# A four-layer network on one core: filler matmuls, earlier centre copies, later x copies and a lent PSUM bank in the scan layer

## The chip, the core and the metric

The kernel runs on one core of one Trainium2 chip. The time is that of one launch on the device in microseconds (us); a comparison uses the median of several runs. The profiles are one profiled execution each: PE is TensorE's matmuls, PEld its weight loads, DVE is VectorE, ACT is ScalarE, POOL is GpSimd, and SP is the engine from whose queue the scan layer's DMAs are issued. "L1800" is line 1800 of the kernel.

## What is computed

The input `x` has shape 3 x 256 x 48 x 48 in float32. Four layers follow one another, each of the form `x = x + layer(groupnorm(x))`: an attention block, a convolution whose weights are mixed per image, a plain 3x3 convolution, and a selective state-space scan (Mamba). The change is in the fourth layer. With L = 2304 tokens per image it is, cut to what matters:

```
xn = layernorm(tokens, over channels) * norm_w + norm_b
x_in, z = split(xn @ in_proj_w.T)               # 512 channels each
u  = silu(conv1d(x_in, 4 taps per channel) + conv_b)
dt_raw, B, C = split(u @ x_proj_w.T)            # 16, 16, 16
dt = softplus(dt_raw @ dt_proj_w.T + dt_proj_b)
for each token t:                               # 16 states per channel
    h = h * exp(dt_t * A) + dt_t * B_t * u_t
    y_t = sum over states of h * C_t
y   = (y + u * D) * silu(z)
out = y @ out_proj_w.T                          # 256 channels
```

## The kernel before, in words

**Chunks, steps and parts.** Of each image's 2304 tokens 384 are a chunk (CH), so there are 3 x 6 = 18 chunks. The 512 inner channels are four groups of 128 (m = 0 to 3), the 16 states of a channel two halves (h = 0, 1). A pair (m, h) is a step, so that a chunk has 8 steps, called 0 to 7 here (step = 2m + h); "steps five to eight" of the change are steps 4 to 7 in this count. A step has 8 parts, each one scan of 128 rows by 384 tokens. There are 18 x 8 x 8 = 1152 scans. "Scan (2, 3)" is part 3 of step 2, and so for the exponentials.

**What one part does.** `scan` (L1797) is one VectorE instruction (L1800). It multiplies the running state by the decay in a PSUM slot and adds the tile `hs`. The decay is `exp(dt * A)`, written by ScalarE in `decay` (L1784, instruction L1792). There are three slots, so the exponential for a part is issued three parts ahead, after the scan that frees its slot: after scan (2, 0) follows exponential (2, 3).

**What one step does.** At its end `fill` (L1754) writes the inputs `dt * u * B` of the next step into `hs`. VectorE writes the upper part (`fill_upper`, L1745, instruction L1748) and reads `dt * u` from a PSUM tile of two banks that TensorE has spread over the rows (`spread_pe`, L1712). GpSimd writes the rest (L1762, L1766) from rows that DMAs have spread (`spread`, L1693; `spread_second`, L1704). Then GpSimd multiplies the finished states by C (`times_c`, L1804, instruction L1817), and TensorE adds them up one step later (`add_states`, L1822). `gate` (L1839) multiplies the sum by silu(z) on VectorE. `spread_pe` runs at the end of even steps and has one tile: the banks are written at the end of step 2m - 2, both are read at the end of step 2m - 1, and the first one once more at the end of step 2m.

**What is threaded in between.** All other work of the layer is cut into small stages that run beside the scans of other chunks. Three lists say where: `plan` (L1381) for the chunks one and two ahead, `gating` (L1430) for z, `after` (L1418) for the chunk before. An entry `(j, place, rel, stage)` runs `stage` for chunk `at + rel` in half step j (j = 2 x step + part // 4) at a place: BEGIN, MID, DONE and LATE are after the first, second, third and fourth scan of the half step, and PE_ is after LATE in its first half and after `fill` and `times_c` in its second. Within a place the order is `after`, `plan`, `gating`, `last_of_all`. The lines that matter:

- `group_scale` (L1210), `less_mean` (L1218: TensorE, both shared banks), `centre` (L1233: two ScalarE copies L1235 out of the banks and a Square L1237), `square_mean` (L1227), `inverse_root` (L1239: Ln L1241 and Exp L1242), `normalise` (L1244, VectorE), `tokens` (L1248): the layer norm of the chunk two ahead, in steps 6 and 7.
- `project_x` (L1261), `take_x` (L1268: ScalarE copy L1269), `taps` (L1271: 8 records L1273), `take_u` (L1278: ScalarE L1281), in steps 0 to 2, and `silu` (L1285) over u in step 3. `silu` over z is `last_of_all`, at (3, LATE). Each silu is a table load, the pass over 1536 columns (L1286) and a table load back (L229).
- `project_u`, `take_dbc`, `project_dt` (L1315), `softplus`, `take_dt` (L1331: VectorE L1334, L1335), `keep_dt` (L1337: ScalarE copies L1339 and two stores), in steps 4 to 6.
- `project_z`, `take_z` (L1354, L1357) in steps 6 and 7 and at the start of the next chunk.
- `residual` (L1368), `project_y` (L1359: 10 records, L1361 and L1363), `store` (L1372: ScalarE copy L1373 and a DMA): the output of the chunk before. It is made in two halves of 128 channels.

All stages share two PSUM banks, `bank[0]` and `bank[1]` (L1206): each product lies there until ScalarE or VectorE has taken it.

**What sets the order.** TensorE, VectorE, ScalarE and GpSimd run the layer's instructions in program order (`keep_order`, L1906). An instruction that waits holds up all behind it on its engine. SP's DMAs are ordered by the framework and wait for their own semaphores; they are often issued well ahead of the compute beside them. The loop over steps and parts is at L1853 to L1890, the end of the layer (last sum, gate, output) at L1892 to L1901.

Of the kernel before, what the change touches and what calls it, by code (L numbers as in the profile page):

```python
# [16 lines left out]
P = 128  # L17
# [8 lines left out]
CH = 384  # L26
# [9 lines left out]
DI = 4  # L36
# [48 lines left out]
def net(  # L85
# [21 lines left out]
    nc = tc.nc  # L107
# [14 lines left out]
    def v(name, i=0, n=1):  # L122
# [3 lines left out]
    ident = const.tile([P, P], F32, name="ident")  # L126
# [6 lines left out]
        out=gview, in_=gview, pattern=[[-8, 16], [0, 8]], compare_op=ALU.is_ge,  # L133
# [3 lines left out]
        out=gview, in_=gview, pattern=[[8, 16], [0, 8]], compare_op=ALU.is_ge,  # L137
# [243 lines left out]
    with ExitStack() as l0:  # L381
# [36 lines left out]
        with ExitStack() as p1:  # L418
# [15 lines left out]
            for b in ORDER:  # L434
# [100 lines left out]
        with ExitStack() as p2:  # L535
# [9 lines left out]
            for i in range(NB):  # L545
# [501 lines left out]
        i = NB - 1  # L1047
# [151 lines left out]

    class Chunk:  # L1200
        def __init__(self):
            self.second = {}


    whole = [psg.tile([P, 512], F32, name=f"ps_g{j}") for j in range(2)]
    bank = [t[:, :CH] for t in whole]  # L1206
# [61 lines left out]
    def take_x(k, m):  # L1268
        nc.scalar.copy(w3v["xi"][:, m % 3, :], whole[m % 2][:, :XH])  # L1269

    def taps(k, m):  # L1271
        for tap in range(DCONV):
            nc.tensor.matmul(  # L1273
                bank[m % 2], w3v["taps"][:, m, tap, :], w3v["xi"][:, m % 3, tap : tap + CH],
                start=tap == 0, stop=tap == DCONV - 1,
            )

    def take_u(k, m):  # L1278
        if m == 0:
            k.u = room(k, "u")  # L1280
        nc.scalar.activation(  # L1281
            k.u[:, m, :], bank[m % 2], AF.Identity, bias=v("conv_b", m)
        )
# [39 lines left out]
    def softplus(k, m0):  # L1323
# [4 lines left out]
        nc.scalar.activation(both, both, AF.Exp, scale=-1.0)  # L1328
        nc.scalar.activation(both, both, AF.Ln, bias=1.0)

    def take_dt(k, m0):  # L1331
        for j in range(2):
            m, pdt = m0 + j, bank[j]
            nc.vector.scalar_tensor_tensor(pdt, pdt, 0.0, k.dt[:, m, :], ALU.max, ALU.add)  # L1334
            nc.vector.tensor_tensor(k.dtu[:, m, :], pdt, k.u[:, m, :], ALU.mult)  # L1335

    def keep_dt(k, m0):  # L1337
        for j in range(2):
# [17 lines left out]
            k.sz = room(k, "sz")  # L1356
        nc.scalar.copy(k.sz[:, m, :], bank[j])  # L1357

    def project_y(k, mo, lo=0, hi=DI):  # L1359
        if lo == 0:  # L1360
            nc.tensor.matmul(bank[mo], ident, k.ot[:, mo, :], start=True, stop=False)  # L1361
        for m in range(lo, hi):
            nc.tensor.matmul(  # L1363
                bank[mo], w("out", m * 256 + mo * P, P), k.sz[:, m, :],
                start=False, stop=m == DI - 1,
            )

# [2 lines left out]
        nc.sync.dma_start(k.ot, xd[k.b][:, :, k.c * CH : (k.c + 1) * CH])  # L1370

    def store(k, mo):  # L1372
        nc.scalar.copy(k.ot[:, mo, :], bank[mo])  # L1373
        nc.sync.dma_start(
            out[k.b, mo * P : (mo + 1) * P, k.c * CH : (k.c + 1) * CH], k.ot[:, mo, :]
        )
# [3 lines left out]
    BEGIN, MID, DONE, LATE, PE_ = range(5)  # L1380
    plan = [  # L1381
        (12, MID, 2, group_scale),
        (12, PE_, 2, less_mean),
        (13, LATE, 2, centre),
        (13, PE_, 2, square_mean),
        (14, MID, 2, inverse_root),
        (15, MID, 2, normalise),
# [8 lines left out]
        (2, DONE, 1, lambda k: project_x(k, 2)),  # L1396
        (2, LATE, 1, lambda k: take_u(k, 1)),
        (2, LATE, 1, lambda k: project_x(k, 3)),
        (3, LATE, 1, lambda k: take_x(k, 2)),
        (3, LATE, 1, lambda k: taps(k, 2)),  # L1400
        (4, BEGIN, 1, lambda k: take_x(k, 3)),
        (4, BEGIN, 1, lambda k: taps(k, 3)),
        (4, DONE, 1, lambda k: take_u(k, 2)),
        (5, MID, 1, lambda k: take_u(k, 3)),
        (7, LATE, 1, lambda k: silu(k.u)),
        (8, BEGIN, 1, project_u),
        (8, LATE, 1, take_dbc),
# [11 lines left out]
        (0, MID, 0, lambda k: k.at and take_z(k, 2, 0)),  # L1419
        (0, MID, 0, lambda k: k.at and take_z(k, 3, 1)),  # L1420
        (2, MID, -1, residual),
        (5, BEGIN, -1, lambda k: project_y(k, 0)),
        (6, MID, -1, lambda k: store(k, 0)),
        (7, PE_, -1, lambda k: project_y(k, 1)),
        (8, MID, -1, lambda k: store(k, 1)),
    ]

    last_of_all = [(3, LATE, 0, lambda k: silu(k.sz))]

# [246 lines left out]
    with ExitStack() as l3:  # L1676
# [35 lines left out]
        def spread_pe(k, m):  # L1712

            t = psr.tile([P, 2, 512], F32, name="ps_r")
            for q in range(2):
                r = slice(32 * q, 32 * q + 32)
                nc.tensor.matmul(
                    t[:, q, :CH], rep[r].rearrange("p r d -> p (r d)"), k.dtu[r, m, :],
                    start=True, stop=True,
                )  # L1720
            k.ps = t


        steps = [(at, m, h) for at in range(len(todo)) for m in range(DI) for h in range(2)]
        tiles = {}
        state = {}

        parts_of_step = [(g, q) for a in range(2) for g in range(2) for q in (2 * a, 2 * a + 1)]
        slots = [psd.tile([P, 512], F32, name=f"ps_da{i}") for i in range(3)]
# [54 lines left out]
        def decay(n):  # L1784

            s, part = divmod(n, 8)
            if s >= len(steps):
                return
            at, m, h = steps[s]
            g, q = parts_of_step[part]  # L1790
            col = (m * 4 + 2 * h + g) * 4 + q
            nc.scalar.activation(  # L1792
                slots[n % 3][:, 1 : CH + 1], chunks[at].rows[m][0][:, q, :], AF.Exp,
                scale=amat[:, col : col + 1],
            )
# [49 lines left out]
        k = chunks[0]  # L1845
# [7 lines left out]
        for s, (at, m, h) in enumerate(steps):  # L1853
            if m == 0 and h == 1 and at + 2 <= last:
                fetch(at + 2)
            for part in range(8):
                j = 4 * m + 2 * h + part // 4
                scan(s, part)
                decay(8 * s + part + 3)
                if part == 0 and h == 0:  # L1860
                    c, n = (at, m + 1) if m + 1 < DI else (at + 1, 0)
                    if c <= last:
                        rows = getattr(chunks[c], "rows", {})
                        chunks[c].rows = {**rows, n: spread(chunks[c], n)}
                if part == 4 and h == 1 and s + 1 < len(steps):
                    spread_second(chunks[steps[s + 1][0]], steps[s + 1][1])
                if part == 4 and s + 1 < len(steps):
                    first_states(s + 1)
                if part % 4 == 0:
                    run(at, j, BEGIN)  # L1870
                if part % 4 == 1:
                    run(at, j, MID)
                if part % 4 == 2:
                    run(at, j, DONE)
                if h == 1 and part == 7 and s >= 3:
                    gate(*steps[s - 3][:2])
# [139 lines left out]
```

## Time and profile before

| | |
|---|---|
| time, median of 3 runs | 3412.58 us (3409.98 to 3416.41) |
| the profiled execution, its own time | 3411.51 us |
| its span, first to last instruction | 3409.8 us |
| its scan stage, first to last scan | 2018.1 to 3389.4 us |
| VectorE busy from 2018.0 to 3389.4 us | 1318.6 of 1371.4 us |
| GpSimd busy there | 1271.2 us |
| ScalarE busy there | 1101.1 us |
| TensorE busy there, mean granted clock | 1091.5 us, 0.87 |
| after the last scan, to the end | 20.4 us |

A line of the timeline gives start, duration, engine, source line, operation, output<-inputs and shape, how many equal instructions are merged, and in brackets the engine's idle time before and what ended it. The view of waits sums such brackets by who waited for whom. The view by windows gives each engine's busy time in stretches of time, and "PEclk", the share of full speed that TensorE was granted. A float32 matmul of the kernel's text appears as two records, each with its own weight load.

### The profile page before, as it was taken

What the parts mean: (1) busy time and instruction counts of PE and PEld (TensorE: products, weight loads), DVE (VectorE), ACT (ScalarE), POOL (GpSimd) and SP (SyncE); (2) the same over time, 40 slices, a digit from 0 to 9 for tenths busy, and PEclk for the clock granted to TensorE, in tenths of its full rate; (3) what the DMA queues carried; (4) which work ended last, traced back from release to release, by engine and by line L of the source; (5) the groups of instructions that cost most, each with busy time, mean ns of one, the idle gap of its engine ahead of it and who ended that gap; (6) DMA issues with size and microseconds to landing.
All of it is one profiled execution on the core that took longest, in us unless ns stands there. A gap on an engine that the chain in (4) does not pass through costs nothing.

```text
span 3409.8 us, 52160 instructions
## 1 busy us (share of the span) xinstructions
PE 3047.4 (89%) x19882; PEld 1442.5 (42%) x19882; DVE 2902.4 (85%) x3302; ACT 2381.6 (70%) x3596; POOL 1335.5 (39%) x457
## 2 busy tenths in 40 slices
PE   7999999999999999979999987878888888878785
PEld 4334343453333435547677753333333333333331
DVE  3799889959989996479966369999999999999998
ACT  2688888848888885332233558888888888888874
POOL 0000000000000000210000039999899999999897
PEclk8999999999999999989999998888889898988887
DMA  4000000010000002756501144545555454545552
GB/s 167 28 8 10 8 8 7 12 42 5 8 10 8 7 8 80 238 171 222 199 22 38 42 116 110 120 115 139 141 126 131 121 122 121 128 114 136 137 133 54
DMA packets 182152, 290.65 MB, mean 85 GB/s; under 512 B 34737, under 2 KB 148465, under 8 KB 179970
## 3 DMA queue, kind: packets, MB, share of 16 engines
q1 hardware_dynamic: 168658, 267.15, 29.0%
q10 hardware_dynamic: 13232, 20.06, 1.8%
q8 instruction: 158, 2.59, 0.3%
q14 instruction: 104, 0.85, 0.1%
HBM read 236.24 MB, written 50.64 MB: 84 GB/s over the span
## 4 chain that ended last, share of the span: by engine, by line
PE 59%; DVE 21%; ACT 11%; DMA 4%; issue 3%; POOL 1%; SPq 1%; ACTq 0%; DVEq 0%; POOLq 0%
PE ps_s L638 16%; PE acc L651 14%; DVE hs L1800 13%; PE ps_c L1533 8%; PE ps_g L1273 3%; PE ps_g L1222 3%; ACT ps_da L1792 2%; DVE u L296 2%; PE ps_y L462 2%; PE ps_m L665 1%; PE ps_s L1031 1%; PE ps_m L711 1%; PE ps_y L1834 1%; PE ps_g L1349 1%; ACT L229 1%
## 5 line engine op out<-in xcount | busy, mean ns | idle before, releaser
L642 ACT ACTIVATE pt<-ps_s 128x1024 f32<-128x1024 f32 x972 | 942.6, 1022 | 154.5 <-PE ps_s L638 141.8
L1800 DVE TENSOR_TENSOR_SCAN hs<-ps_da,hs 128x385 f32<-128x385 f32 x1152 | 1006.6, 940 | 47.4 <-ACT ps_da L1792 45.8
L857 DVE TENSOR_TENSOR part<-part,pt 128x2048 f32<-128x2048 f32 x396 | 906.8, 2290 | 41.2 <-ACT pt L642 18.4
L1792 ACT ACTIVATE ps_da<-dtr,u 128x384 f32<-128x384 f32 x1152 | 657.0, 583 | 201.7 <-DVE hs L1800 191.0
L164 POOL TENSOR_TENSOR rstd<-ve,mhalf 128x2 f32<-128x2 f32 (+1 forms) x26 | 16.4, 631 | 1476.5 <-DVE ve L162 1476.5
L638 PE MATMUL ps_s<-q,kt 32*128 32x512 f32 (+1 forms) x4320 | 576.4, 592 | 0.1
L651 PE MATMUL acc<-pt,vt 128*32 128x512 f32 (+1 forms) x4320 | 520.9, 561 | 0.2
L1533 PE MATMUL ps_c<-vt,u 128*128 128x288 f32 x1728 | 432.5, 411 | 21.0 <-DVE u L263 21.0
L1817 POOL TENSOR_TENSOR hc<-hs,x 128x3072 f32<-128x3072 f32 x72 | 405.3, 5629 | 5.4 <-DVE hs L1800 5.2
L1817 POOL TENSOR_TENSOR hc<-hs,bc 128x3072 f32<-128x3072 f32 x71 | 399.8, 5631 | 11.0 <-DVE hs L1800 7.9
L1533 PEld LDWEIGHTS ps_c<-vt,u 128*128 128x128 f32 x1728 | 331.0, 192 | 117.6 <-issue 19.8
L638 PEld LDWEIGHTS ps_s<-q,kt 32*128 32x128 f32 x4320 | 195.3, 183 | 199.1 <-issue 120.2
L1834 PE MATMUL ps_y<-hc,u 128*32 128x384 f32 x2304 | 252.0, 562 | 17.3 <-POOL hc L1817 17.3
L651 PEld LDWEIGHTS acc<-pt,vt 128*32 128x32 f32 x4320 | 94.4, 108 | 353.4 <-issue 326.7
L1273 PE MATMUL ps_g<-u 128*128 128x384 f32 x576 | 199.5, 494 | 21.0 <-ACT u L1269 20.9
L1766 POOL TENSOR_TENSOR hs<-dtur,x 128x1536 f32<-128x1536 f32 x72 | 209.2, 2905 | 7.2 <-DMA dtur<-dtud 7.2
L1766 POOL TENSOR_TENSOR hs<-dtur,bc 128x1536 f32<-128x1536 f32 x72 | 209.6, 2911 | 0.0
L1318 PE MATMUL ps_g<-wconv,u 17*128 17x384 f32 x144 | 79.2, 684 | 106.7 <-ACT x L1339 81.0
L1273 PEld LDWEIGHTS ps_g<-u 128*128 128x128 f32 x576 | 107.0, 190 | 110.5 <-ACT u L1269 42.2
L1222 PE MATMUL ps_g<-wconv,u 128*128 128x384 f32 x144 | 85.6, 765 | 64.6 <-ACT x L1339 64.1
L1834 PEld LDWEIGHTS ps_y<-hc,u 128*32 128x32 f32 x2304 | 65.4, 119 | 178.8 <-issue 152.6
L1549 ACT COPY cb<-ps_c 128x288 f32<-128x288 f32 x48 | 19.2, 399 | 158.4 <-PE ps_c L1533 144.2
(251 smaller groups left out, 3842.5 us busy)
## 6 DMA issues: line engine op xcount, KB each, us to landing
wconv<-in_we SPq DMA_DIRECT2D x144, 384.0 KB, 4.2
dtr<-dtd SPq DMA_DIRECT2D x288, 192.0 KB, 4.0
dtur<-dtud SPq DMA_DIRECT2D x288, 96.0 KB, 4.2
wconv<-xd SPq DMA_DIRECT2D x36, 384.0 KB, 4.9
x<-bcd SPq DMA_DIRECT2D x72, 192.0 KB, 5.3
dtd<-x SPq DMA_DIRECT2D x36, 384.0 KB, 3.5
dtuq<-dtud SPq DMA_DIRECT2D x288, 48.0 KB, 2.2
bc<-bcd SPq DMA_DIRECT2D x72, 192.0 KB, 5.1
```

The lines of the kernel that those rows point to most:

```text
L638: nc.tensor.matmul(s[:, j, cols], kt[r, mt * P : (mt + 1) * P], q[r, :n], start=True, stop=True,)
L642: nc.scalar.activation(p[:, h0 : h0 + 2, :], s, AF.Exp)
L651: nc.tensor.matmul(acc[h * HD : (h + 1) * HD, :n], vt[:, mt, g * P + h * HD : g * P + (h + 1) * HD], p[:, h, cols], start=mt == 0, stop=mt ...
L857: ): nc.vector.tensor_tensor(part, first, p, ALU.add)
L1222: nc.tensor.matmul(bank[to], w3v["less"][:, int(to != ct), :], k.xg[:, ct, :], start=ct == 0, stop=ct == CT - 1,)
L1273: nc.tensor.matmul(bank[m % 2], w3v["taps"][:, m, tap, :], w3v["xi"][:, m % 3, tap : tap + CH], start=tap == 0, stop=tap == DCONV - 1,)
L1533: nc.tensor.matmul(pc[:, :HN], u[:, i, dy, ct, m * P : (m + 1) * P], vt[:, i, ct, dy * TW : dy * TW + HN], start=ct == 0 and dy == 0, stop ...
L1766: nc.gpsimd.tensor_tensor(states(s)[:, :, 2:4, 1:], chunks[at].rows[m][1].unsqueeze(1).broadcast_to([P, 2, 2, CH]), b_rows(s, 0, 2), ALU.mult,
L1792: nc.scalar.activation(slots[n % 3][:, 1 : CH + 1], chunks[at].rows[m][0][:, q, :], AF.Exp, scale=amat[:, col : col + 1],)
L1800: nc.vector.tensor_tensor_scan(b, slots[(8 * s + part) % 3][:, : CH + 1], b, 0.0, ALU.mult, ALU.add)
L1817: nc.gpsimd.tensor_tensor(hc, tiles[s][:, :, :, 1:], cb.broadcast_to([P, 2, 4, CH]), ALU.mult)
L1834: nc.tensor.matmul(k.y_ps[32 * q : 32 * q + 32, :CH], fold, hc[:, g, q, :], start=False, stop=h == 1 and g == 1,)
```

## The change

- **Fillers.** `keep_busy(src, times)` issues matmuls of 128 columns with the identity as weights. Nobody reads their results. They go to columns 384 to 511 of the two banks of the current spread tile, alternately. They stand at `take_dt` (3 after each product `dtu`, once a spread tile exists), after scan (4, 3): 4; after scans (5, 1), (5, 2), (5, 3), (5, 5): 3 each; after scans (6, 0), (6, 1), (6, 2): 3, 3, 2; and 5 between `less_mean` and `square_mean`, at (13, PE_). Each of the fillers behind a scan reads what that scan wrote.
- **Centre.** `centre` moves from (13, LATE) to (13, DONE), one part earlier.
- **x copies.** `take_x` and `taps` of m = 2 move from (3, LATE) to (4, BEGIN), behind z's silu; those of m = 3 from (4, BEGIN) to (4, DONE). `take_u` of m = 2 moves from (4, DONE) to (5, LATE), of m = 3 from (5, MID) to (6, LATE).
- **First output half.** `project_y(k, 0)` moves from (5, BEGIN) to (4, BEGIN) and is written to the second bank of the spread tile instead of `bank[0]`; its `store` moves from (6, MID) to (5, DONE).
- **Spread rows.** `spread_second` moves from part 4 to part 0 of odd steps.

```
+    def keep_busy(src, times):
+        for i in range(times if spread_tiles else 0):
+            nc.tensor.matmul(
+                spread_tiles[-1][:, i % 2, CH:], ident, src, start=True, stop=True
+            )
...
     def take_dt(k, m0):
...
             nc.vector.tensor_tensor(k.dtu[:, m, :], pdt, k.u[:, m, :], ALU.mult)
+            keep_busy(k.dtu[:, m, :P], 3)
...
-    def project_y(k, mo, lo=0, hi=DI):
+    def project_y(k, mo, lo=0, hi=DI, into=None):
         if lo == 0:
-            nc.tensor.matmul(bank[mo], ident, k.ot[:, mo, :], start=True, stop=False)
+            k.y_out[mo] = bank[mo] if into is None else into
+            nc.tensor.matmul(k.y_out[mo], ident, k.ot[:, mo, :], start=True, stop=False)
...
     def store(k, mo):
-        nc.scalar.copy(k.ot[:, mo, :], bank[mo])
+        nc.scalar.copy(k.ot[:, mo, :], k.y_out[mo])
...
-        (13, LATE, 2, centre),
+        (13, DONE, 2, centre),
+        (13, PE_, 2, lambda k: keep_busy(ident, 5)),
         (13, PE_, 2, square_mean),
...
-        (3, LATE, 1, lambda k: take_x(k, 2)),
-        (3, LATE, 1, lambda k: taps(k, 2)),
-        (4, BEGIN, 1, lambda k: take_x(k, 3)),
-        (4, BEGIN, 1, lambda k: taps(k, 3)),
-        (4, DONE, 1, lambda k: take_u(k, 2)),
-        (5, MID, 1, lambda k: take_u(k, 3)),
+        (4, BEGIN, 1, lambda k: take_x(k, 2)),
+        (4, BEGIN, 1, lambda k: taps(k, 2)),
+        (4, DONE, 1, lambda k: take_x(k, 3)),
+        (4, DONE, 1, lambda k: taps(k, 3)),
+        (5, LATE, 1, lambda k: take_u(k, 2)),
+        (6, LATE, 1, lambda k: take_u(k, 3)),
...
-        (5, BEGIN, -1, lambda k: project_y(k, 0)),
-        (6, MID, -1, lambda k: store(k, 0)),
+        (4, BEGIN, -1, lambda k: project_y(k, 0, 0, DI, lent[0])),
+        (5, DONE, -1, lambda k: store(k, 0)),
...
     def spread_pe(k, m):
...
             k.ps = t
+            lent[0] = t[:, 1, :CH]
+            spread_tiles[:] = [t]
...
+        busy = {(2, 0, 3): 4, (2, 1, 1): 3, (2, 1, 2): 3, (2, 1, 3): 3, (2, 1, 5): 3,
+                (3, 0, 0): 3, (3, 0, 1): 3, (3, 0, 2): 2}
...
                 scan(s, part)
                 decay(8 * s + part + 3)
+                if (m, h, part) in busy:
+                    g, q = parts_of_step[part]
+                    keep_busy(tiles[s][:, g, q, 1 : P + 1], busy[m, h, part])
...
-                if part == 4 and h == 1 and s + 1 < len(steps):
+                if part == 0 and h == 1 and s + 1 < len(steps):
                     spread_second(chunks[steps[s + 1][0]], steps[s + 1][1])
```

More of the change, by code (lines that the diff above doesn't have):

```diff
@@ L1201, in __init__ @@
         def __init__(self):
-            self.second = {}
+            self.second, self.y_out = {}, {}
     whole = [psg.tile([P, 512], F32, name=f"ps_g{j}") for j in range(2)]
@@ L1329, in softplus @@
         nc.scalar.activation(both, both, AF.Ln, bias=1.0)
+    spread_tiles = []
+    def keep_busy(src, times):
[3 more added lines that the diff above has]
+            )
     def take_dt(k, m0):
@@ L1357, in take_z @@
         nc.scalar.copy(k.sz[:, m, :], bank[j])
-    def project_y(k, mo, lo=0, hi=DI):
+    def project_y(k, mo, lo=0, hi=DI, into=None):
         if lo == 0:
-            nc.tensor.matmul(bank[mo], ident, k.ot[:, mo, :], start=True, stop=False)
+            k.y_out[mo] = bank[mo] if into is None else into
+            nc.tensor.matmul(k.y_out[mo], ident, k.ot[:, mo, :], start=True, stop=False)
         for m in range(lo, hi):
             nc.tensor.matmul(
-                bank[mo], w("out", m * 256 + mo * P, P), k.sz[:, m, :],
+                k.y_out[mo], w("out", m * 256 + mo * P, P), k.sz[:, m, :],
                 start=False, stop=m == DI - 1,
@@ L1426, in net @@
     ]
+    lent = [None]
     last_of_all = [(3, LATE, 0, lambda k: silu(k.sz))]
```

## The prediction

> **What bounds the kernel now.** I read the busy table by windows first: from the first to the last scan (1371.4 us) VectorE is busy for 1318.6. So the stage is VectorE's, and all that a schedule can win is its idle time, 53 us. The view of waits of VectorE in that stage says whose it is; I then looked up each such wait in the timeline.
>
> ```profile
> DVE hs L1800 <- ACT ps_da L1792: 45.8, 50, 1.4
> ```
>
> 50 waits of a scan for its exponential, 45.8 us. They stand at three places of a chunk: before scan (2, 3), 1.13 us in 17 chunks (18.7 in all); before (7, 3), 1.38 and 0.3 in turn in 16 chunks (14.0); before (7, 5), 0.75 in 16 chunks (12.2). First step 2, ScalarE, then VectorE:
>
> ```profile
> 2494.90 0.59 ACT L1792 ACTIVATE ps_da<-dtr,u 128x384 f32<-128x384 f32 x1 [0.27 <-DVE hs L1800]
> 2496.22 0.48 ACT L1269 COPY u<-ps_g 128x387 f32<-128x387 f32 x1 [0.74 <-PE ps_g L1263]
> 2496.72 1.28 ACT L1286 ACT_TABLE_LOAD   x1
> 2498.01 1.49 ACT L1286 ACTIVATE x<-x 128x1536 f32<-128x1536 f32 x1
> 2499.52 1.28 ACT L229 ACT_TABLE_LOAD   x1
> ...
> 2500.92 0.58 ACT L1792 ACTIVATE ps_da<-dtr,u 128x384 f32<-128x384 f32 x1
> ```
> ```profile
> 2497.75 2.66 DVE L1800 TENSOR_TENSOR_SCAN hs<-ps_da,hs 128x385 f32<-128x385 f32 x3
> 2501.53 2.77 DVE L1800 TENSOR_TENSOR_SCAN hs<-ps_da,hs 128x385 f32<-128x385 f32 x3 [1.13 <-ACT ps_da L1792]
> ```
>
> Exponentials (2, 2) and (2, 3) are 6.0 us apart. Between them lie z's silu, a copy of x, and ScalarE's wait of 0.74 for the matmuls behind that copy. Three slots let ScalarE lead by three scans; that isn't enough. Then step 7 (ScalarE, TensorE, VectorE):
>
> ```profile
> 2544.72 0.58 ACT L1792 ACTIVATE ps_da<-dtr,u 128x384 f32<-128x384 f32 x1 [0.26 <-DVE hs L1800]
> 2545.77 0.48 ACT L1235 COPY wconv<-ps_g 128x384 f32<-128x384 f32 x1 [0.46 <-PE ps_g L1222]
> 2547.05 0.48 ACT L1235 COPY wconv<-ps_g 128x384 f32<-128x384 f32 x1 [0.80 <-PE ps_g L1222]
> 2547.56 0.84 ACT L1237 ACTIVATE wconv<-wconv 128x768 f32<-128x768 f32 x1
> ...
> 2548.40 1.09 ACT L1792 ACTIVATE ps_da<-dtr,u 128x384 f32<-128x384 f32 x2
> 2550.05 0.56 ACT L1241 ACTIVATE ps_g<-ps_g,epst 128x384 f32<-128x384 f32 x1 [0.56 <-PE ps_g L1229]
> ```
> ```profile
> 2541.52 5.49 PE L1222 MATMUL ps_g<-wconv,u 128*128 128x384 f32 x8 [4.17 <-ACT x L1339]
> 2548.45 0.91 PE L1229 MATMUL ps_g<-wconv,mean 128*128 128x384 f32 x2 [1.45 <-ACT wconv L1237]
> ```
> ```profile
> 2549.08 1.81 DVE L1800 TENSOR_TENSOR_SCAN hs<-ps_da,hs 128x385 f32<-128x385 f32 x2 [1.38 <-ACT ps_da L1792]
> 2551.64 0.96 DVE L1800 TENSOR_TENSOR_SCAN hs<-ps_da,hs 128x385 f32<-128x385 f32 x1 [0.75 <-ACT ps_da L1792]
> ```
>
> The centre copies wait for `less_mean`, 8 records in 5.49 us, 0.64 apart; at full clock records of this size are 0.32 apart. The windows view shows why: after TensorE's pauses of steps 5 and 6 the granted clock is half.
>
> ```profile
> 2523.25:2536.90 13.65, 9.63 (x38) 2.97 (x30) 13.40 (x18) 10.97 (x23) 13.14 (x4) 0.50 0.41 98
> 2540.30:2547.10 6.80, 5.49 (x8) 2.52 (x8) 6.80 (x10) 4.77 (x11) 4.01 (x3) 0.50 1.08 249
> ```
>
> (Columns after the length: PE, PEld, DVE, ACT and POOL busy, then the clock.)
>
> **What the Trainium skill says.** (1) "TensorE: Matmul & The Clock Gate", section "What's actually happening": TensorE runs at half clock after an idle window of about 3.4 us and at full clock after a busy one. The trace agrees: 0.64 against 0.32 us per record, and stretches of a multiple of 3.4 us. (2) "PSUM — Partial Sum Buffer", section "PSUM bank collisions raise a hardware error": two engines must be kept apart by bank, not by address. So I take a filler and the `fill_upper` that reads another part of its bank to be ordered by a wait. No pair in this trace shows it. (3) "ScalarE: Activation LUTs", "What ACT_TABLE_LOAD costs": about 1283 ns a load; here 1.28.
>
> **Part by part.**
>
> *x copies behind the silu.* Exponential (2, 2) ends at 2495.49. Without copy and wait the table load starts at 2495.5, 1.2 us sooner, and exponential (2, 3) ends at 2500.3 instead of 2501.5. VectorE is ready at 2501.53 - 1.13 = 2500.40. The wait falls from 1.13 to 0.1. The copy (0.47) now stands behind (2, 3): (2, 4) ends about 2501.2, when VectorE wants it; the second copy, after (2, 5), has 0.4 us of slack. I leave 0.1 us per chunk (ends 0 and 0.4): **17 x 1.0 = 17 us won**.
>
> *Output half in the lent bank, taps, later u copies.* TensorE's work in step 2 is the same, in another order: sums (from 2497.3 to 2499.4), `project_y` 10 x 0.32 to 2502.6, taps 8 x 0.32 each to 2505.2 and 2507.8. Those who take the results come later: the store's copy at about 2504.4, the u copies at 2505.4 and 2508.6. The lent bank was last read by `fill` at the end of step 1 and is next written by the spread at the end of step 2, behind the taps, at about 2509 as before (2509.5); it is needed 4 us later. Cost 0; without that slack the u copies would hold ScalarE for tenths. The residual's DMA gets behind `spread_second` on SP, hence behind GpSimd's L1762 (2485.6): it lands by 2493 for use at 2499.4. Nothing. The store's own DMA only moves forward.
>
> *Spread rows sooner.* Their four issues stood behind a store of step 5 and eight loads of B and C; GpSimd waited 4.5 us for them in step 6 (59.9 and 22.5 us in all by the waits view). VectorE didn't: L1766 ends at 2546.8 and its first reader is scan (7, 4) at 2549.96. Worth 0 directly, but it gives GpSimd (71.3 us of work in 76.4 us) the room for a shorter chunk. On SP the stores of `keep_dt` get behind these issues, which wait for GpSimd's L1762: done by 2521.1, the stores are ready at 2530.8. Nothing.
>
> *Fillers.* A filler is two records of 128 columns: a third of 0.32, so 0.11 us each if streaming binds; 0.19 each if the weight load does (a load of 128 columns has a mean of 190 ns in group L1273). So 3 fillers are 0.6 to 1.1 us. To count activity I take streaming time times the share of the array used. In the trace, windows of 3.4 us under about 0.25 turned the clock down, those over 0.3 didn't, and 0.7 turned it up. The pauses get 3 x 0.21 = 0.64 us after nearly every scan: six groups in step 5 and five in step 6, at most 1.8 us apart except around the sums of step 4's states, which are 1.9 us of work themselves (2 x 0.32 and 4 x 0.32). Every window then holds 0.4 or more by this count. I take the clock to stay up. Then `less_mean` ends 2.6 us sooner (8 x 0.32).
>
> A filler waits for its scan or product, and all of TensorE's queue behind it with it: `project_dt` and `less_mean`. Both wait longer for ScalarE's copies of the banks; the last fillers before `less_mean` follow scan (6, 2), which ends at 2540.4, so they end 0.4 us before it can start. But `fill` at the end of step 5 reads both their banks: `project_dt` from 2530.45, 4 records to 2532.0, 3 fillers to 2532.6 to 2533.1; `fill` starts at 2533.13, with all of step 6's scans behind it on VectorE. I take 0.05 us, ends 0 and 0.3: **1 us lost**.
>
> *Centre one part earlier.* Exponential (7, 1) ends at 2544.47. `less_mean` gives its banks by 2544.4, so copies and Square (1.75 us) run without a wait to 2546.1, (7, 2) ends at 2546.65; VectorE wants it at 2546.77. The margin is 0.1 us. (7, 3) ends at 2547.3, wanted 2547.6. **All of 14.0 us won.** Next late is (7, 5): it stands behind Ln and Exp (0.98 us), which wait for `square_mean`, 1.6 us after its start (2548.45 to 2550.05). Square ends at 2546.1, but the five fillers in front start only after `fill` has read their bank (2545.1) and take 1.1 to 1.9 us, to 2546.3 to 2547.0; `square_mean`, z's product and the next sums queue behind them. So Ln starts at 2547.9 to 2548.6, (7, 5) ends at 2549.5 to 2550.2, wanted 2549.3. I take 0.5 left of 0.75 (ends 0.2 and 0.9): **4 us won** (ends +9 and -2).
>
> Sum: 17 + 14 + 4 - 1 = 34 us. The profiled execution took 3411.5 (span 3409.8 and 1.7 around it): 3377.5. The median of the runs is 1.1 above it: **3378.6 us**. With all ends good it is 3371, with all bad 3394. The 20.4 us after the last scan hold no edit.
>
> **Rivals.**
>
> *All hidden.* If a filler's record takes 0.11 us and starts ahead of `fill`'s read, Ln isn't held up: nearly all 45.8 us go, 3367.
>
> *Step 7 keeps its waits.* For: the margin of 0.1 us at (7, 2), and five fillers ahead of `square_mean`. What is won at (7, 3) comes back at (7, 2) and (7, 5); step 2 alone remains: 3412.6 - 17 = 3396.
>
> *The clock stays down, and the change costs time.* One mechanism, at the pauses of steps 5 and 6: fillers count for too little, and a window under a quarter halves the clock. Then `less_mean` frees its second bank at 2547.05, as before; Square ends at 2548.4, (7, 2) at 2549.0 against 2546.8, so 2.2 in one phase, 1.3 in the other (where the clock had risen halfway), instead of 0.85 at (7, 3). Fillers at half clock (0.43 or more) and `square_mean` (4 x 0.64) add about 1.1 at (7, 5). So 16 x (0.9 + 1.1) = 32. `fill` of step 5 waits for `project_dt` to 2533.2 and 3 fillers to 2534.5: 17 x 1.4 = 24. Less 17 from step 2: 3412.6 + 39 = 3452. Against it: the counted windows. It decides from 0.25 down.
>
> *No effect.* GpSimd, with 5 us to spare per chunk, becomes the bound and returns what VectorE wins: 3411. Against it: its wait for rows goes.
>
> **Chances.** As forecast 0.60, all hidden 0.13, step 7 keeps its waits 0.15, clock down 0.09, no effect 0.03. The likeliest case alone reaches from 3371 to 3394; the range for 8 in 10 takes in the two cases beside it, 3364 to 3400. A measurement of this kernel can tell about 0.2% (7 us) from no change. Faster 0.88, same 0.03, slower 0.09.
>
> **What would show it.** Right: no wait over 0.15 us before scan (2, 3) and none at (7, 3); a clock of 1.00 all through steps 4 to 7; `less_mean` in 2.9 us; some 0.5 us left at (7, 5); GpSimd's wait for `dtuq` gone. Wrong: waits before scan (7, 2), a `fill` of VectorE waiting for TensorE, windows at 0.50, waits for GpSimd's `hs`.

## The result, and the profile after

| | before | after |
|---|---|---|
| median of 4 runs each | 3411.28 us | 3373.68 us (3369.03 to 3375.2) |
| ratio, 95% interval | | 0.9885 [0.9869, 0.99] |
| the profiled execution | 3411.51 us | 3369.03 us |
| its layers ahead of the scans | 2018.1 | 2013.8 |
| its scan stage, start of the first to end of the last scan | 1371.3 | 1330.8 |
| from there to the end | 20.4 | 22.7 |

37.6 us are won by the medians. The profiled execution of after happens to be the shortest of its four runs. Of its 42.5 us, 4.3 lie in layers whose code is unchanged: in all the executions shown here the first scan starts anywhere from 2012.9 to 2022.0 us. So each kernel below is read by its ratio and by its scan stage. The stage is shorter by 40.5 us.

From L1331 on, line numbers move by up to 17: the scan is L1817 now, the exponential L1809, `fill_upper` L1765, GpSimd's fills L1779 and L1783, the store's copy L1384, a filler L1336. The view of waits of VectorE, from 2000 us on, shows who waited for whom, us in all, how often and the longest:

```profile
DVE sz L1858 <- PE ps_y L1851: 7.8, 1, 7.8
DVE hs L1765 <- ACT wconv L1384: 3.6, 17, 0.2
...
DVE ps_g L1343 <- ACT x L1329: 3.0, 17, 0.2
...
DVE hs L1817 <- ACT ps_da L1809: 2.4, 3, 1.6
```

50 waits of 45.8 us for an exponential have become 3 of 2.4, all in the first chunk; waits of 0.09 us that remain at (7, 5), too short for this view, come to 1.4 us more. The first line is the gate after the last scan. The second is new: 17 waits of `fill_upper` for the store's copy.

**Step 2 after the change**, ScalarE, then VectorE, in the timeline of one chunk:

```profile
2476.69 0.58 ACT L1809 ACTIVATE ps_da<-dtr,u 128x384 f32<-128x384 f32 x1 [0.27 <-DVE hs L1817]
2477.29 1.28 ACT L1286 ACT_TABLE_LOAD   x1
2478.59 1.48 ACT L1286 ACTIVATE x<-x 128x1536 f32<-128x1536 f32 x1
2480.09 1.28 ACT L229 ACT_TABLE_LOAD   x1
2481.38 0.20 ACT L1799 COPY gmat<-hs 128x8 f32<-128x8 f32 x1
2481.49 0.58 ACT L1809 ACTIVATE ps_da<-dtr,u 128x384 f32<-128x384 f32 x1
...
2485.76 0.58 ACT L1809 ACTIVATE ps_da<-dtr,u 128x384 f32<-128x384 f32 x1 [0.27 <-DVE hs L1817]
2486.28 0.47 ACT L1384 COPY wconv<-ps_r 128x384 f32<-128x384 f32 x1
```
```profile
2479.55 7.02 DVE L1817 TENSOR_TENSOR_SCAN hs<-ps_da,hs 128x385 f32<-128x385 f32 x8
2486.78 0.56 DVE L1765 TENSOR_TENSOR hs<-ps_r,x 128x384 f32<-128x384 f32 x1 [0.21 <-ACT wconv L1384]
```

The table load follows exponential (2, 2) at once, (2, 3) starts 4.8 us after (2, 2) instead of 6.0, and the eight scans run without a gap. But the last scan ends at 2486.57, the store's copy only at 2486.75, and `fill_upper` starts 0.03 us after that. `fill_upper` reads the first bank of the spread tile, the copy the second, where the output half now lies.

**Step 7 after the change**, TensorE, ScalarE, VectorE:

```profile
2522.40 2.85 PE L1222 MATMUL ps_g<-wconv,u 128*128 128x384 f32 x8 [0.31 <-ACT x L1349]
2526.07 1.38 PE L1336 MATMUL ps_r<-ident 128*128 128x128 f32 x10 [0.83 <-DVE hs L1765]
2527.29 1.46 PE L1229 MATMUL ps_g<-wconv,mean 128*128 128x384 f32 x4
```
```profile
2524.75 0.58 ACT L1809 ACTIVATE ps_da<-dtr,u 128x384 f32<-128x384 f32 x1 [0.27 <-DVE hs L1817]
2525.27 0.85 ACT L1235 COPY wconv<-ps_g 128x384 f32<-128x384 f32 x2
2526.15 0.84 ACT L1237 ACTIVATE wconv<-wconv 128x768 f32<-128x768 f32 x1
2526.90 0.57 ACT L1809 ACTIVATE ps_da<-dtr,u 128x384 f32<-128x384 f32 x1
...
2528.78 0.56 ACT L1241 ACTIVATE ps_g<-ps_g,epst 128x384 f32<-128x384 f32 x1 [0.20 <-PE ps_g L1229]
```
```profile
2525.48 0.53 DVE L1765 TENSOR_TENSOR hs<-ps_r,x 128x384 f32<-128x384 f32 x1
2525.93 5.40 DVE L1817 TENSOR_TENSOR_SCAN hs<-ps_da,hs 128x385 f32<-128x385 f32 x6
```

`less_mean` takes 2.85 us (5.49 before) and ends as ScalarE comes to the centre copies, so copies, Square and exponential (7, 2) follow one another without a wait. The ten filler records ahead of `square_mean` wait 0.83 us for `fill_upper`, which ends at 2526.01. They write other columns of the bank that it reads. The Trainium skill ("PSUM — Partial Sum Buffer", section "PSUM bank collisions raise a hardware error") asks for engines to be kept apart by bank; after shows a wait that fits it. But in step 2 `fill_upper` also waited for a reader of the other bank of the same tile, so no run here tells whether the order is kept by bank or by tile. The records then take 1.22 us for ten, 0.12 us each, and `square_mean` starts 0.3 us after Square's end. Six scans in 5.40 us hold 0.09 us of waiting, at (7, 5).

**The clock.** The windows view of the same chunk, steps 5 and 6 (columns: length; PE, PEld, DVE, ACT, POOL busy; granted clock; DMA share; GB/s):

```profile
2506.00:2511.00 5.00, 4.29 (x30) 3.68 (x30) 4.76 (x8) 3.40 (x8) 5.00 (x2) 1.00 1.02 226
2511.00:2516.00 5.00, 4.50 (x19) 1.95 (x21) 5.00 (x7) 4.58 (x11) 4.72 (x2) 0.85 0.96 246
2516.00:2521.00 5.00, 4.87 (x38) 3.01 (x31) 4.93 (x8) 3.29 (x6) 5.00 (x3) 0.81 0.00 0
2521.00:2526.00 5.00, 3.93 (x16) 2.21 (x15) 5.00 (x8) 4.31 (x10) 2.38 (x2) 1.00 0.50 147
```

Not all windows hold: one of 3.4 us is at half clock here, from 2514.49 us. The window ahead of it and the window itself:

```profile
2511.08:2514.49 3.41, 2.91 (x13) 1.70 (x12) 3.41 (x6) 3.05 (x8) 3.13 (x2) 1.00 1.08 236
2514.49:2517.90 3.41, 3.41 (x18) 0.59 (x16) 3.41 (x4) 2.72 (x6) 3.41 (x1) 0.50 0.30 121
```

From 2030 to 3270 us the time at half clock is 27.3 us (eight such windows), before it was 279.9.

GpSimd's fills waited for the spread rows before (59.9 us for `dtuq`, and 22.5 us in waits that the view puts down to ScalarE). One such wait is left:

```profile
POOL hs L1783 <- DMA dtuq<-dtud: 0.9, 1, 0.9
```

### The profile page after: what moved, and what is told of

The parts are those of the page before. It is cut to its first block, busy times and chain, and to the rows that moved or that the text cites. A ratio compares the mean times of both kernels' runs of the same rounds, so it can differ in the third digit from the quotient of the medians.

```text
span 3367.3 us, 54979 instructions
## 1 busy us (share of the span) xinstructions
PE 3151.7 (94%) x21314; PEld 1586.5 (47%) x21314; DVE 2899.6 (86%) x3302; ACT 2375.1 (71%) x3596; POOL 1335.3 (40%) x457
## 4 chain that ended last, share of the span: by engine, by line
PE 52%; DVE 32%; ACT 7%; DMA 4%; issue 4%; SPq 1%; POOL 0%; ACTq 0%; DVEq 0%; POOLq 0%
DVE hs L1817 21%; PE ps_s L638 16%; PE acc L651 14%; PE ps_c L1546 8%; DVE hs L1765 3%; DVE u L296 2%; PE ps_y L462 2%; PE ps_m L665 2%; ACT ps_da L1809 2%; PE ps_s L1031 2%; PE ps_m L711 1%; PE acc L529 1%; PE ps_s L518 1%; DVE ps_g L1343 1%; DMA dtr<-dtd 1%
## 5 line engine op out<-in xcount | busy, mean ns | idle before, releaser
L1817 DVE TENSOR_TENSOR_SCAN hs<-ps_da,hs 128x385 f32<-128x385 f32 x1152 | 1002.6, 936 | 5.1 <-ACT ps_da L1809 2.4
L1809 ACT ACTIVATE ps_da<-dtr,u 128x384 f32<-128x384 f32 x1152 | 656.3, 582 | 191.3 <-DVE hs L1817 182.7
L1851 PE MATMUL ps_y<-hc,u 128*32 128x384 f32 x2304 | 228.1, 516 | 2.8 <-POOL hc L1834 2.8
L1783 POOL TENSOR_TENSOR hs<-dtur,x 128x1536 f32<-128x1536 f32 x72 | 209.0, 2903 | 8.3 <-DMA dtur<-dtud 8.3
L1783 POOL TENSOR_TENSOR hs<-dtur,bc 128x1536 f32<-128x1536 f32 x72 | 209.3, 2907 | 1.3 <-DMA dtuq<-dtud 0.9
L1336 PE MATMUL ps_r<-hs,ident 128*128 128x128 f32 x864 | 130.9, 292 | 27.3 <-DVE hs L1817 27.2
L1336 PEld LDWEIGHTS ps_r<-hs,ident 128*128 128x128 f32 x864 | 107.6, 192 | 80.8 <-DVE hs L1817 63.0
```

Source lines behind the costliest of these rows:

```text
L1336: nc.tensor.matmul(spread_tiles[-1][:, i % 2, CH:], ident, src, start=True, stop=True)
L1783: nc.gpsimd.tensor_tensor(states(s)[:, :, 2:4, 1:], chunks[at].rows[m][1].unsqueeze(1).broadcast_to([P, 2, 2, CH]), b_rows(s, 0, 2), ALU.mult,
L1809: nc.scalar.activation(slots[n % 3][:, 1 : CH + 1], chunks[at].rows[m][0][:, q, :], AF.Exp, scale=amat[:, col : col + 1],)
L1817: nc.vector.tensor_tensor_scan(b, slots[(8 * s + part) % 3][:, : CH + 1], b, 0.0, ALU.mult, ALU.add)
L1851: nc.tensor.matmul(k.y_ps[32 * q : 32 * q + 32, :CH], fold, hc[:, g, q, :], start=False, stop=h == 1 and g == 1,)
```

## The experiments

**Theory:** the scan stage shortens by what VectorE's waits shorten by. The moves of x win (2, 3), the fillers keep the clock up and so win (7, 3), the sooner centre wins (7, 5), and the lent bank takes a little back. **Rivals:** the moves do the work and the fillers nothing; the fillers do it all; the five fillers ahead of `square_mean` are what keeps step 7 fast; the sooner spread rows give the room for a shorter chunk.

The edits are made in after, unless a part is put back as before. Each ratio is to runs of before taken together with that kernel (medians 3411.28 to 3413.21 us). The table sums, for each kernel, VectorE's waits by their place over all chunks (us), as worked out from its trace, the time at half clock in stretches that begin from 2030 to 3270 us, and the scan stage. "fill 3" is the wait of `fill_upper` ahead of step 3's scans, "fill 6" ahead of step 6's. Sums under 1 us stand as 0 (after still has 0.4 us at (2, 3), in its first chunk).

| kernel | (2,3) | fill 3 | fill 6 | (7,2) | (7,3) | (7,5) | half clock | scan stage |
|---|---|---|---|---|---|---|---|---|
| before | 18.7 | 0 | 0 | 0 | 14.0 | 12.2 | 280 | 1371.3 |
| after | 0 | 3.6 | 0 | 0 | 0 | 1.4 | 27 | 1330.8 |
| no fillers | 0 | 3.6 | 0 | 21.1 | 0 | 1.1 | 266 | 1351.9 |
| fillers alone | 18.7 | 0 | 1.6 | 0 | 0 | 12.1 | 27 | 1358.3 |
| x copies back | 18.6 | 0 | 0 | 0 | 0 | 1.4 | 14 | 1345.4 |
| centre late | 0 | 3.6 | 0 | 0 | 0 | 12.1 | 3 | 1340.9 |
| without the five | 0 | 3.6 | 0 | 0 | 0 | 0 | 21 | 1328.1 |
| store sooner | 0 | 0 | 0 | 0 | 0 | 1.5 | 14 | 1325.8 |
| one filler each | 0 | 3.6 | 15.7 | 22.3 | 0 | 1.2 | 270 | 1372.4 |
| sooner, tail filled | 0 | 0 | 0 | 0 | 0 | 1.5 | 14 | 1326.8 |
| rows late | 0 | 3.6 | 0 | 0 | 0 | 1.4 | 24 | 1331.1 |
| two fillers each | 0 | 3.6 | 4.3 | 0 | 0 | 0 | 133 | 1332.1 |
| all of the best | 0 | 0 | 0 | 0 | 0 | 0 | 21 | 1323.2 |

**No fillers.**

```
-        for i in range(times if spread_tiles else 0):
+        for i in range(0):
```

> All moves of the change, no filler. Theory of the forecast (the fillers hold TensorE's clock, and the early centre copies pay only then): the clock falls to 0.5 in steps 5 and 6 as before. The wait before scan (2, 3) is gone (17 us won). In step 7 the centre copies wait for the slow less_mean, now ahead of exponential (7, 2): a wait of 1.3 and 2.2 us in turn before scan (7, 2) in place of 0.85 and 0.75 before (7, 3) and (7, 5), so nothing won there. The new wait of 0.21 us before step 3 stays. Total 3398. Rival (the moves do it all, the clock does not matter): 3374, as with fillers.

Measured: 3394.2 us (3392.12 to 3398.42), ratio 0.9945 [0.9928, 0.9962]: 18.9 us faster than before, 20 slower than after by the medians. The view of waits of VectorE:

```profile
DVE hs L1817 <- ACT ps_da L1809: 22.5, 18, 2.1
...
DVE hs L1765 <- ACT wconv L1384: 3.6, 17, 0.2
```

The moves win (2, 3) without any filler. In step 7 the sooner centre at half clock only moves the wait: 26.1 us at (7, 3) and (7, 5) become 21.1 at (7, 2) and 1.1. That is 18.7 + 3.9 - 3.6 = 19 us, the time measured. Half of the gain needs the clock.

**Fillers alone.** All moves put back as before, the fillers kept.

```
-        (13, DONE, 2, centre),
+        (13, LATE, 2, centre),
...
-        (4, BEGIN, 1, lambda k: take_x(k, 2)),
-        (4, BEGIN, 1, lambda k: taps(k, 2)),
+        (3, LATE, 1, lambda k: take_x(k, 2)),
+        (3, LATE, 1, lambda k: taps(k, 2)),
...
-        (4, BEGIN, -1, lambda k: project_y(k, 0, 0, DI, lent[0])),
-        (5, DONE, -1, lambda k: store(k, 0)),
+        (5, BEGIN, -1, lambda k: project_y(k, 0)),
+        (6, MID, -1, lambda k: store(k, 0)),
...
-                if part == 0 and h == 1 and s + 1 < len(steps):
+                if part == 4 and h == 1 and s + 1 < len(steps):
```

> The kernel before with the fillers alone: no stage is moved. Theory: clock 1.00 in steps 4 to 7, less_mean in 2.9 us. The wait before (2, 3) stays at 1.13 us in 17 chunks. Before (7, 3) it falls from 0.85 to 0.1, since the copies find their banks full; before (7, 5) it stays at 0.8, since Square ends later than with the early centre. Total 3411 - 12 = 3399. Rival (fillers hold up VectorE through the shared banks): 3415 or more, with fills of VectorE waiting for TensorE.

Measured: 3398.42 us (3395.93 to 3402.52), ratio 0.9958 [0.9941, 0.9974].

```profile
DVE hs L1817 <- ACT ps_da L1809: 32.9, 35, 1.7
```

35 waits instead of 50: the 16 at (7, 3) are gone (14.0 us), those at (2, 3) and (7, 5) stay to the tenth. So neither half stands for the whole, and they are not a plain sum. In the trace's waits the moves alone win 19 us and the fillers alone 14.0 - 1.6 + 0.1 = 12.5, both together 39.5. Of the 8 us between, 6.8 are in step 7, where (7, 5) needs the sooner centre and the clock at once; most of the rest is the single wait of 1.6 at "fill 6".

**x copies back.** `take_x`, `taps`, `take_u` and the first output half as before; fillers, centre and rows as in after.

```
-        (4, BEGIN, 1, lambda k: take_x(k, 2)),
+        (3, LATE, 1, lambda k: take_x(k, 2)),
...
-        (4, BEGIN, -1, lambda k: project_y(k, 0, 0, DI, lent[0])),
-        (5, DONE, -1, lambda k: store(k, 0)),
+        (5, BEGIN, -1, lambda k: project_y(k, 0)),
+        (6, MID, -1, lambda k: store(k, 0)),
```

> The changed kernel with the x copies, taps, u copies, first output half and its store back at their old places and bank. Theory (silu's burst is what delays (2, 3)): the wait of 1.1 us before (2, 3) is back in 17 chunks, 18.7 us, and the 0.21 us before step 3 (3.6 us, from the lent bank) is gone; step 7 stays without waits. Total 3374 + 15 = 3389. Rival (the wait before (2, 3) hung on the clock or on GpSimd): it stays away, 3370.

Measured: 3387.25 us (3385.34 to 3391.8), ratio 0.9922 [0.9906, 0.9939]. The first line of its waits:

```profile
DVE hs L1817 <- ACT ps_da L1809: 20.9, 19, 1.8
```

17 of them, 18.6 us, are the wait at (2, 3), which is back; the one of `fill_upper` for the store is gone (3.6). This part of the change nets 15 us in the trace, 14 by the medians. The new wait comes with this part; "store sooner" below narrows it down to the store's copy out of the lent bank.

**Centre late.**

```
-        (13, DONE, 2, centre),
+        (13, LATE, 2, centre),
```

> The changed kernel with centre back at (13, LATE). Theory: at full clock the copies no longer wait, so only 0.1 us before (7, 3); but Square ends 0.8 us later, so Ln and with it exponential (7, 5) are late: 0.8 us before (7, 5) in 16 chunks. Total 3374 + 14 = 3388. Rival (with the clock up the place of centre is free): 3374.

Measured: 3381.62 us (3376.95 to 3387.21), ratio 0.9909 [0.9892, 0.9926]. The wait view has 18 waits in place of 3:

```profile
DVE hs L1817 <- ACT ps_da L1809: 13.6, 18, 1.2
```

16 of them stand at (7, 5), 0.75 us each, and none at (7, 3): with the clock up, the centre isn't late at (7, 3) at its old place either. So the fillers won all of (7, 3), and the sooner centre won (7, 5) alone, 10.6 us by the trace. The ratio's interval overlaps that of after; the 8 us between the medians agree with the trace, and don't show it by themselves.

**Without the five.**

```
-        (13, PE_, 2, lambda k: keep_busy(ident, 5)),
```

> The changed kernel without the five fillers between less_mean and square_mean. Theory (they stand in square_mean's way and the clock does not need them): square_mean starts 0.3 us sooner, the 0.09 us before (7, 5) goes, the clock stays at 1.00 in step 7: 3372, no change that can be told. Rival (the pause between the two products turns the clock down): windows at 0.5 in step 7 or 0, square_mean and z's products at half speed, 3380 to 3390.

Measured: 3370.36 us (3368.61 to 3373.77), ratio 0.988 [0.9863, 0.9896]; half clock 21 us instead of 27. The last 1.4 us at (7, 5) go, the stage is 2.7 us shorter, and the clock stays up as in after. These five hold nothing that the others don't; they are the whole of the wait that was left there.

**Store sooner.**

```
-        (5, DONE, -1, lambda k: store(k, 0)),
+        (5, MID, -1, lambda k: store(k, 0)),
```

> The changed kernel with the first output half's store one part earlier, at (5, MID). Theory (VectorE's fill at the end of step 2 waits for ScalarE's copy out of the lent tile): the wait of 0.21 us before step 3 goes in 17 chunks, 3.6 us: 3370. Rival (something else ends that wait, or ScalarE waits for project_y and delays the exponentials): 3374 or more.

Measured: 3367.19 us (3367.06 to 3371.83), ratio 0.9873 [0.9856, 0.9889]. The line "hs L1765 <- ACT wconv L1384" is absent from its waits, and from the first scan of step 2 to the first of step 3 it takes 7.41 us at the median instead of 7.71. Again the intervals overlap; the lines decide. One part sooner, the copy is done before the last scan ends:

```profile
2482.22 7.04 DVE L1817 TENSOR_TENSOR_SCAN hs<-ps_da,hs 128x385 f32<-128x385 f32 x8
2489.18 0.53 DVE L1765 TENSOR_TENSOR hs<-ps_r,x 128x384 f32<-128x384 f32 x1
```

Here `fill_upper` starts 0.08 us before the record of the last scan ends, as VectorE's instructions do when nothing holds them up (0.08 or 0.09 us). A wait loses this overlap too, so 0.21 us of idle time cost 0.30: the stage is 5.0 us shorter, not 3.6, and "without the five" 2.7, not 1.4.

**One filler each.** Every group of fillers, the five too, is cut to one matmul.

```
-        for i in range(times if spread_tiles else 0):
+        for i in range(1 if spread_tiles else 0):
```

> The changed kernel with one filler wherever it has two to five. Theory (the clock follows the share of the array used per window of 3.4 us, down at about 0.25): groups of 0.21 us every 0.9 to 1.1 us make 0.2, so the clock falls in steps 5 and 6 in most chunks, and the time is near that of the moves without fillers, 3395. Rival (any activity that leaves no pause of 3.4 us holds the clock): 3373.

Measured: 3414.39 us (median of 12 runs, 3407.32 to 3419.47), ratio 1.0003 [0.9995, 1.0012]. The expectation missed by 19 us, its rival by 41. Fewer fillers are 20 us slower than none at all. Its waits:

```profile
DVE hs L1817 <- ACT ps_da L1809: 24.8, 19, 2.0
DVE hs L1765 <- PE ps_r L1336: 15.7, 17, 0.9
```

The clock is down as often as without fillers (270 and 266 us), so step 7 waits at (7, 2) as there. The second line is what fillers add. TensorE, then VectorE, ahead of step 6's scans:

```profile
2532.51 2.92 PE L1318 MATMUL ps_g<-wconv,u 17*128 17x384 f32 x4 [0.23 <-ACT x L1349]
2535.36 0.80 PE L1336 MATMUL ps_r<-hs,ident 128*128 128x128 f32 x2
```
```profile
2536.19 2.62 DVE L1765 TENSOR_TENSOR hs<-ps_r,x 128x1536 f32<-128x1536 f32 x2 [0.92 <-PE ps_r L1336]
```

At half clock `project_dt` takes 2.92 us. The filler behind it ends at 2536.16, and `fill_upper`, which reads the filler's bank, starts 0.03 us later. Without fillers `project_dt` takes as long, but nobody on VectorE waits for it:

```profile
2523.77 2.92 PE L1318 MATMUL ps_g<-wconv,u 17*128 17x384 f32 x4 [5.48 <-ACT x L1349]
2526.62 1.65 PE L1846 MATMUL ps_y<-x,diag 128*128 128x384 f32 x2
```

A filler ties the bank that it writes to all of TensorE's queue ahead of it; with the clock up that is free, with the clock down it costs 0.92 us a chunk.

**Two fillers each.**

```
-        for i in range(times if spread_tiles else 0):
+        for i in range(min(times, 2) if spread_tiles else 0):
```

> The changed kernel with at most two fillers at each place. Theory (activity counted as share of the array and the window, down at about 0.25): groups of 0.43 us make 0.35 to 0.4 of a window, so the clock holds in nearly all chunks: 3374. Rival (the bound lies nearer to what three fillers give, 0.5): the clock falls in most chunks, the fill before step 6 waits for TensorE as with one filler, 3405 to 3415.

Measured: 3372.61 us (3370.61 to 3378.34), ratio 0.9885 [0.9869, 0.9902]. The time is as expected, the reason isn't: the clock does not hold in nearly all chunks. It is at half for 133 us, and where it falls in step 5 `fill_upper` waits for fillers, up to 1.5 us:

```profile
DVE hs L1765 <- PE ps_r L1336: 4.3, 6, 1.5
```

Of these 4.3 us, 1.4 come back at (7, 5), where two fillers hold `square_mean` up less than five; the stage is 1.3 us longer than after's. Step 7 needs only that the clock has risen again by then: `less_mean` takes at most 2.85 us in every chunk.

**Rows late.**

```
-                if part == 0 and h == 1 and s + 1 < len(steps):
+                if part == 4 and h == 1 and s + 1 < len(steps):
```

> The changed kernel with spread_second back at part 4 of odd steps. Theory of the forecast (GpSimd's wait for these rows never reaches VectorE): GpSimd waits some 4 us for dtuq in step 6 again, VectorE waits for no more of GpSimd's hs than with the change; 3374. Rival (with a shorter chunk GpSimd has no room left): waits of scans for GpSimd's hs in step 7, 0.3 to 1 us per chunk, 3380 to 3390.

Measured: 3375.28 us (3367.11 to 3376.81), ratio 0.9892 [0.9875, 0.9908]. GpSimd waits for its rows again, in several lines of its waits, the largest of which is

```profile
POOL hs L1779 <- DMA dtuq<-dtud: 30.7, 8, 5.5
```

and VectorE waits for GpSimd twice:

```profile
DVE hs L1817 <- POOL hs L1783: 1.4, 2, 0.9
```

The sooner rows are worth nothing that can be measured here; even at 74.3 us a chunk GpSimd has the slack.

**Store sooner, and the tail filled.** Three fillers more behind each scan of the very last step.

```
-        (5, DONE, -1, lambda k: store(k, 0)),
+        (5, MID, -1, lambda k: store(k, 0)),
...
                     keep_busy(tiles[s][:, g, q, 1 : P + 1], busy[m, h, part])
+                elif at == last and m == DI - 1 and h == 1:
+                    g, q = parts_of_step[part]
+                    keep_busy(tiles[s][:, g, q, 1 : P + 1], 3)
```

> The changed kernel with the store at (5, MID) and three fillers behind each scan of the last step of all, so that the clock is up when the last sums, gate and output begin. Theory: 3.6 us from the store, and the stretch after the last scan falls from 22.7 us to about 18.5: 3366. Rival (the end is bound by VectorE's last product and by the DMA out, not by the clock): only the store's part, 3370.

Measured: 3365.89 us (3360.49 to 3371.69), ratio 0.9863 [0.9845, 0.988]. The windows view of its last microseconds, then of after's:

```profile
3338.00:3345.00 7.00, 5.75 (x48) 4.53 (x40) 7.00 (x10) 3.93 (x7) 7.00 (x3) 1.00 0.02 5
3345.00:3352.00 7.00, 7.00 (x42) 4.04 (x42) 4.77 (x5) 0.00 (x0) 1.49 (x1) 1.00 0.00 0
```
```profile
3337.00:3344.00 7.00, 2.02 (x16) 0.33 (x8) 7.00 (x10) 3.58 (x7) 7.00 (x3) 0.51 0.01 2
3344.00:3351.00 7.00, 5.93 (x21) 2.13 (x22) 5.14 (x4) 0.00 (x0) 1.85 (x1) 0.52 0.01 2
```

The clock is full where it was half, but the time after the last scan falls only to 20.4 us (22.7 in after, 21.5 with the store sooner alone). From the last scan to the last gate it is 9.9 us instead of 12.4, so the clock does pay there. Fillers hold TensorE for 0.8 us after the last scan, ahead of the last sum: its first matmul starts at 3346.73, the scan ends at 3345.90.

```profile
3346.73 0.81 PE L1846 MATMUL ps_y<-u,diag 128*128 128x384 f32 x2
```

From the last gate to the end it is 8.9 to 10.7 us in the thirteen traces, 10.5 here, so the filled tail wins nothing behind the gate.

**All of the best.** Store sooner, without the five, the tail filled.

```
-        (13, PE_, 2, lambda k: keep_busy(ident, 5)),
...
-        (5, DONE, -1, lambda k: store(k, 0)),
+        (5, MID, -1, lambda k: store(k, 0)),
...
+                elif at == last and m == DI - 1 and h == 1:
+                    g, q = parts_of_step[part]
+                    keep_busy(tiles[s][:, g, q, 1 : P + 1], 3)
```

> The changed kernel with the store at (5, MID), without the five fillers ahead of square_mean, and with three fillers behind each scan of the last step of all. Theory (the three are independent): 3.6 us before step 3, 1.5 us before (7, 5), 1 to 2 us after the last scan: 3367.5. Rival (the clock falls in step 7 without the five when the rest is faster): 3375 or more.

Measured: 3363.39 us (3362.41 to 3364.36), ratio 0.9857 [0.984, 0.9873]: 10.3 us below after by the medians, the shortest here. The trace accounts for 10.1 of them: the stage is 7.6 us shorter and the tail 2.5 (20.2 after the last scan). The waits that went, 3.6 for the store and 1.4 for the five, are only 5.0 of the 7.6; the rest is the overlap lost with each of these 33 waits (33 x 0.08 = 2.6). 3367.5 was expected, and most of the 4 us between are this overlap.

## Why the prediction held, and where its steps failed

34 us were forecast for the profiled execution and 37.6 were measured by the medians. The places and their causes were right, most of the sizes too; but that the sum comes so near is in part luck, since a term that was too small at (7, 5) and two losses that were put at nothing, the lent bank and the tail, partly cancel. In the trace the terms came out as follows.

- **(2, 3): right.** 17 us forecast, 18.3 won; the 0.1 us a chunk that were left over are a margin (0.05 us in the chunk shown), not a wait.
- **(7, 3): right, by one of its two reasons.** 14.0 forecast and won. The step named the sooner centre; "centre late" shows that with full clock the old place has no wait at (7, 3) either. The clock did it.
- **(7, 5): mechanism right, size wrong.** 4 us forecast, 10.8 won. The term that was mis-sized is the price of five fillers: I had 0.11 to 0.19 us a record and took the middle; ten records took 1.22 us, 0.12 each, which fits streaming (a third of 0.32) and not the weight load, though each has one of 0.19 us in the trace. What is left is 0.09 us a chunk, not 0.5, and "without the five" shows those fillers as its cause. That brings the time toward "all hidden" (3367), half of whose premise held: 0.12 us a record, but behind the read of `fill_upper`, not ahead of it.
- **"Cost 0" for the lent bank: failed.** 3.6 us lost. The step looked at who writes the bank next and when the tile is read by `fill` at the end of step 1, and not at the `fill_upper` of step 2's end, which reads the tile's other bank and was ordered behind the store's copy. "Store sooner" shows the cost and that it needn't be.
- **`fill` at the end of step 5: overstated.** 1 us forecast, no wait found with the fillers as they are. The pair is real all the same: it is the 15.7 us of "one filler each".
- **The tail:** 20.4 us was carried over; it came to 22.7. Of the 2.3 us, 0.9 lie ahead of the last gate, where the clock is at half for longer (12.4 us instead of 11.5), and 1.4 behind it, where TensorE's last product takes 1.56 us in both; what makes these 1.4 stays open. No edit lies there, and among the executions with an unfilled tail it is 20.4 to 23.3.

So 18.3 + 14.0 + 10.8 - 3.6 = 39.5 us of waits, in a stage that is 40.5 shorter, less 2.3 in the tail. The forecast summed idle time alone, without the overlap that each wait loses.

**The clock's bound was wrong, and did no harm.** The forecast had windows under about 0.25 turning it down, those over 0.3 not, and every window of after at 0.4 or more. By the same count (streaming time times the share of the array) the window of after at 2511.08 holds four records of 0.32 us on 17 of 128 rows (0.17), six of filler (0.64) and one of a sum (0.32), 1.13 of 3.41 us or 0.33, and turns it down. PE's own busy time doesn't show it: 2.91 of 3.41 us. In "two fillers each" 23 of the 25 windows that turn it down lie at 0.24 to 0.38; in before, windows of 0.29 to 0.37 held now and then, which is why the bound looked lower there. Over all thirteen traces, from 2030 to 3265 us, none of 161 windows that turned it down is above 0.39, and 99% of those that held are at 0.39 or more. The Trainium skill ("TensorE: Matmul & The Clock Gate", section "What's actually happening") ties half clock to an idle window of about 3.4 us. The length agrees with the traces; that the window be idle does not: a third of the array's time is not enough. Three fillers to a pause are not generous but near the least.

**The slower rival was a real mechanism at another dose.** "One filler each" is that rival: waits at (7, 2) of 0.84 and 1.95 us in turn where it had 1.3 and 2.2, and of `fill_upper` for fillers of 0.92 where it had 1.4. Its 3452 was too high, mainly because it also added to the wait at (7, 5): a VectorE that has already waited at (7, 2) no longer does there (0.07 us a chunk). "No effect" by way of GpSimd fell: its wait for rows can come back and nothing changes.

**Open.** Why `fill_upper` waits for a copy that reads the other bank of the same tile: both are reads, and it was not tried with two tiles of one bank. The exact bound of the clock: 0.29 to 0.39 lies on both sides by this count, which is itself an estimate. Which of the eight groups of fillers behind scans are needed was not tried one by one. The x copies, the taps, the u copies and the output half were put back only together.

## What to carry to other kernels

When a stage is bound by one engine, list that engine's waits by their place in the repeating unit; each place has its own cause, and the gains by place add up to nearly the stage's (39.5 of 40.5 us here). Filler matmuls pay when they keep the clock up and cost when they don't: here one to a place lost 20 us against none, while five needless ones cost 3. Read the granted clock afterwards, and write fillers to a bank that no busy engine reads soon. A buffer that is lent for a new use needs the list of all who read any part of it next, not only of those who write it.

## What the runs showed of the hardware

- Too few fillers are worse than none: 3414.39 us with one to a place, 3394.2 with none, 3373.68 with those of the change.
- Ten float32 matmul records of 128 columns with the same weights take 1.22 us, 0.12 each, though the weight load of each lasts 0.19 us in the profile.
- A matmul that writes columns 384 to 511 of a bank waited 0.83 us for VectorE's read of columns 0 to 383 of it, and VectorE's read 0.92 us for such a matmul.
- A window of 3.41 us in which TensorE's streaming time, weighted by the share of the array, is a third halved the clock (0.33 at 2511.08 us in after), with PE busy for 2.91 us of it.
- VectorE's instructions overlap by 0.08 or 0.09 us when none waits; an idle time of 0.21 us cost 0.30.
